# A two-layer graph kernel: the sort split by family, the hub's deal moved forward, layer 1 summed in PSUM

## The chip, the cores and the metric

The kernel runs on one core of one Trainium2 chip. The metric is the device time of one execution in microseconds; the median of three executions before the change is 1130.66 us (1130.05 to 1131.23). The profiled execution took 1129.26 us, with a span of 1127.5 us between its first and last instruction.

## The reference

The inputs are 2708 rows of 1024 float32 numbers (`x`) and a 2708 by 2708 adjacency matrix `adj` of zeros and ones. It is sparse: its rows have between none and a few hundred neighbours, most of them a handful.

```python
# layer 0: attention over the neighbours
q = x @ W_q.T + b_q;  k = x @ W_k.T + b_k;  v = x @ W_v.T + b_v
z = (1 / 32) * (q @ k.T)
z = where(z * adj == 0, -10000, z * adj)
x = layernorm(x + relu(softmax(z, axis=1) @ v))
# layer 1: a sum over the neighbours, then a linear layer
x = layernorm(x + adj @ (x @ W) + bias)
```

`layernorm` takes the mean and the variance over the 1024 numbers of a row, with no weights.

## The kernel before, in words

The kernel uses the sparsity. It finds for each row the list of its neighbours, sorts the rows by their number of neighbours, and handles them in 22 blocks of 128 rows; the rows of a block then have about the same number of neighbours. `SLOTS[b]` is the number of neighbours that block `b` has room for. Instead of dense products over all rows, a block gathers row `j` of each of its members by an indirect DMA (128 rows of 4 KB, 0.52 MB), once for each slot.

The unsorted rows fall in two families, sorted each for itself: the first 1024 rows (`FAMILY = 8` blocks, 0 to 7, slots 15 down to 2) and the other 14 blocks (8 to 21, slots 13 down to 0). Rows with very many neighbours ("hub" rows, at most 32) do not fit 15 slots: their neighbours are dealt out over 128 shares of 11 slots each (`HUB_SLOTS`), handled as one more block called "hub" and added to block 0.

The stages, by the order of TensorE's work:

1. The weights are transposed, and `M = W_q.T W_k` is formed (L293, 256 records). A score between two rows is then `(x_i M) . x_j`. `m_sb` holds M.
2. Beside M, `list_columns` finds the neighbours of one block of rows, in unsorted order: VectorE multiplies the rows of `adj` with the column numbers (L217) and takes the largest eight of a range at a time (MAX8, L220 and L222, with replacements L224). 15 of the 22 lists (`EARLY`) are done in M's loop, the others two at a time ahead of a y block.
3. `sort_begin` (L374 to L394) counts, and puts each row in a class by its number of neighbours (L389, then one-hot columns `hot_f`, L393). `sort_end` (L396 to L433) asks TensorE for the running counts (two products, L398 and L400), works out each row's place, and stores each row's record (its neighbours, own number and degree) at that place: 22 indirect scatters of GpSimd into `tab_d` (L428). `tabs` is that table, read back (L433). `records_back` (L435 to L451) derives from it which slots are valid, one slot per instruction (L446, L447, L450, L451): `valid` is 1 or 0, and `less` is 0 or -1e30, which is added to scores.
4. `y_block(b)` computes `y = x M` for 128 rows (L337, 48 records, about 13.85 us), adds a row vector on the way out of PSUM (`yo`, L341) and stores it. The first eight come before any attention, the other 14 between attention steps.
5. The attention of a block is a "job", cut in pieces of at most six slots (`attend`, `run_job`): gather the block's y rows and its neighbours' x rows, one dot product each on VectorE (L593), a softmax over the slots, and the weighted sum of the gathered rows into `r` (L648 for the first, L650 for the others). A step "v" then transposes `r` (`flip`, L521) and multiplies it with `W_v` (L544, 32 records); `finish0` adds bias (L686), relu and residual, normalises (`norm`, L574 to L589) and scatters the finished rows to `x1_d`. The list `steps` sets the order of y blocks and v steps, the lists `jobs` and `late_jobs` that of the attention. How many jobs go ahead of a step is set by a running account (`credit`) of estimated VectorE time.
6. `deal_hub` (L711 to L837) deals out the hub rows. It is a generator: each `next(deal)` emits one part of it, at the start of that loop and in steps 0, 4, 5 and 7 (L960). Its main cost is on VectorE: the neighbours of the hub rows are found eight at a time out of 677 columns (L751, L753), and the place of each slot by comparison (L801). TensorE adds counts (L779), and GpSimd gathers `found`, eleven times.
7. Layer 1 takes the blocks in pairs (`units`, L1133). `sum_rows` (L1035) gathers the neighbours out of `x1_d` and sums them on VectorE: the first one scaled by its mask (L1044), the others by a multiply-add (L1046). `turn1` transposes both sums of a pair and forms four differences `S` (L1071 to L1074). `work1` multiplies with W by the Strassen-Winograd scheme: seven half products instead of eight, each of eight records (L1079) into a PSUM bank of its own. The combination of the seven, and the bias, is done by VectorE adds of 512 columns (L1101, L1121, L1125, L1126) with ScalarE copying the first product (L1100). `finish1` adds the residual row `xr` and sums up for the mean in one instruction (L1055), normalises, and scatters to the output. In turn `i` of the loop the sums of unit `i + 2` are begun.

[...] GpSimd issues all gathers and scatters, so a scatter whose rows are not ready holds up the gathers behind it. Where the kernel says `follow(a, b)`, instruction `a` is placed behind `b`; `high_priority` moves an instruction ahead in the scheduler that sets the order within each engine. `p_o` is a pool of PSUM banks of 128 x 512, called `po`.

Of the kernel before, what the change touches and what calls it, by code (L numbers as in the profile page):

```python
# [20 lines left out]
P = 128  # L21
# [58 lines left out]
def sparse_part(ctx, tc, x, xT, adj, wqT, wkT, wvT, bq, bk, bv, w1, b1, out):  # L80
# [23 lines left out]
    tab_d = dram.tile([NBP, REC], I32, name="tab_d")  # L104
# [6 lines left out]
    with es:  # L111
# [61 lines left out]
        own = lists.tile([P, NB], F32, name="own")  # L173

# [24 lines left out]
        loaded, sorted_ = [], []  # L199
# [83 lines left out]

        m_sb = wm_pool.tile([P, DC, YW], F32, name="m_sb", tag="m")
        nc.vector.memset(m_sb[:, :, D:], 0.0)
        nc.vector.tensor_copy(m_sb[:, :, D], u_col)
        done = 0
        for i in range(DC):
            for h in range(NH):
                hs = slice(h * HALF, (h + 1) * HALF)  # L290
                po = p_o.tile([P, HALF], F32, name="po")
                for o in range(DC):
                    nc.tensor.matmul(po, wq_o[:, o, i * P:(i + 1) * P], wk_o[:, o, hs],  # L293
                                     start=(o == 0), stop=(o == DC - 1))
                nc.scalar.copy(m_sb[:, i, hs], po)
                while done < EARLY * (i * NH + h + 1) // (DC * NH):
                    list_columns()
                    done += 1
        y_bc = xa.tile([P, YW], F32, name="y_bc", bufs=1)
        bcast_rows(y_bc, y_col)  # L300
        mm = p_mm.tile([P, HALF], F32, name="mm")
        nc.tensor.matmul(mm[:, :1], ones, bqk, start=True, stop=True)
        nc.vector.memset(y_bc[:, D:], 0.0)
        nc.vector.tensor_copy(y_bc[:, D:D + 1], mm[:, :1])

# [54 lines left out]
        products = []  # L360
# [3 lines left out]
        NKB = NK * NB  # L364
        deg = lists.tile([P, NB], F32, name="deg")
        hot_f = lists.tile([P, NKB], F32, name="hot_f")
        families = [(0, FAMILY), (FAMILY, NB - FAMILY)]

        def by_class(t, b0, nb):

            return t[:, NK * b0:NK * (b0 + nb)].rearrange("p (k b) -> p k b", b=nb)


        def sort_begin():  # L374
            got = lists.tile([P, NB, KEYS], F32, name="got")
            nc.vector.tensor_scalar(got, keys, 0.0, None, op0=ALU.is_gt)
            capn = lists.tile([P, NB], F32, name="capn")
            nc.vector.tensor_reduce(capn, got, AX.X, ALU.add)
            nc.vector.tensor_tensor(capn, capn, cnt, op=ALU.not_equal)
            nc.vector.scalar_tensor_tensor(deg, capn, 10000.0, cnt, op0=ALU.mult, op1=ALU.add)  # L380
            nc.vector.tensor_scalar(capn, neg, 0.0, 1.0e6, op0=ALU.is_gt, op1=ALU.mult)
            nc.vector.tensor_add(deg, deg, capn)

            past = lists.tile([P, NB], F32, name="past")
            nc.vector.tensor_scalar(past, own, float(N), float(NK - 2), op0=ALU.is_ge, op1=ALU.add)
            kk = lists.tile([P, NB], F32, name="kk")
            nc.vector.memset(kk, 0.0)
            for least in CLASSES:
                nc.vector.scalar_tensor_tensor(kk, deg, float(least), kk, op0=ALU.is_ge, op1=ALU.add)  # L389
            nc.vector.tensor_sub(kk, past, kk)  # L390
            for k in range(NK):
                for b0, nb in families:
                    nc.vector.tensor_scalar(by_class(hot_f, b0, nb)[:, k, :], kk[:, b0:b0 + nb], float(k), None,  # L393
                                            op0=ALU.is_equal)  # L394

        def sort_end():  # L396
            before = p_mm.tile([P, HALF], F32, name="mm")
            nc.tensor.matmul(before[:, :NKB], lower, hot_f, start=True, stop=True)  # L398
            total = p_tr.tile([P, 4, P], F32, name="tr").rearrange("p a b -> p (a b)")
            nc.tensor.matmul(total[:, :NKB], ones, hot_f, start=True, stop=True)  # L400
            one_row = lists.tile([P, NKB], F32, name="one_row")
            nc.vector.memset(one_row, 1.0)
            upto = lists.tile([P, NKB], F32, name="upto")
# [3 lines left out]
            nc.vector.tensor_mul(upto, upto, hot_f)  # L407
            pos = lists.tile([P, NB], F32, name="pos")
            for b0, nb in families:
                nc.vector.tensor_reduce(pos[:, b0:b0 + nb], by_class(upto, b0, nb).rearrange("p k b -> p b k"),  # L410
                                        AX.X, ALU.add)
            pos_i = lists.tile([P, NB], I32, name="pos_i")
            nc.vector.tensor_copy(pos_i, pos)  # L413

            rec = lists.tile([P, NB, REC], I32, name="rec")
            nc.vector.memset(rec[:, :, ROW:], 0)
            own1 = lists.tile([P, NB], F32, name="own1")
            nc.vector.tensor_scalar_add(own1, own, 1.0)
            fill = lists.tile([P, NB, ROW], F32, name="fill")
            nc.vector.scalar_tensor_tensor(fill, keys, 0.0, own1.unsqueeze(2).to_broadcast([P, NB, ROW]),  # L420
                                           op0=ALU.is_equal, op1=ALU.mult)
            nc.vector.scalar_tensor_tensor(rec[:, :, 0:ROW], keys, -1.0, fill, op0=ALU.add, op1=ALU.add)
            nc.vector.tensor_copy(rec[:, :, ROW], own)
            nc.vector.tensor_copy(rec[:, :, DEG], deg)
            for b0, nb in families:
                nc.vector.tensor_scalar_add(rec[:, b0:b0 + nb, OFF], own[:, b0:b0 + nb], float(-b0 * P))
            for b in range(NB):
                put = nc.gpsimd.indirect_dma_start(  # L428
                    out=tab_d[:, :], out_offset=bass.IndirectOffsetOnAxis(ap=pos_i[:, b:b + 1], axis=0),
                    in_=rec[:, b, :], in_offset=None)  # L430
                tc.declare_no_dep(put.ins, group="tab", reason="disjoint rows: positions are unique")
                tc.add_to_no_dep_group("tab", put.ins)
            nc.gpsimd.dma_start(out=tabs, in_=tab_d.rearrange("(b p) e -> p b e", p=P))  # L433

        def records_back():  # L435

            put = nc.vector.tensor_copy(tab0, tabs[:, 0, :])
            follow(put, products[-1])
            nc.gpsimd.dma_start(out=tab0[:HUB, :J0], in_=tab_d[HUB:2 * HUB, ROW - J0:ROW])
            nc.gpsimd.dma_start(out=tab0[:HUB, :ROW - J0], in_=tab_d[HUB:2 * HUB, J0:ROW])  # L440
            nc.gpsimd.dma_start(out=tab0[:HUB, ROW:], in_=tab_d[HUB:2 * HUB, ROW:])
            deg0 = lists.tile([P, 1], F32, name="deg0")
            nc.vector.tensor_copy(deg0, tab0[:, DEG:DEG + 1])
            nc.vector.tensor_scalar_add(deg0[:HUB], deg0[:HUB], float(-J0))
            for j in range(J0):
                nc.vector.tensor_scalar(valid0[:, j:j + 1], deg0, float(j), None, op0=ALU.is_gt)  # L446
                nc.vector.tensor_scalar(less0[:, j:j + 1], deg0, float(j), -FAR, op0=ALU.is_le, op1=ALU.mult)  # L447
            nc.vector.tensor_copy(degs, tabs[:, :, DEG])
            for j in range(max(SLOTS[1:])):
                nc.vector.tensor_scalar(valid[:, :, j], degs, float(j), None, op0=ALU.is_gt)  # L450
                nc.vector.tensor_scalar(less[:, :, j], degs, float(j), -FAR, op0=ALU.is_le, op1=ALU.mult)  # L451


        for b in range(FAMILY):
            while done < min(NB, EARLY + 2 * (b + 1)):
                list_columns()
                done += 1
            y_block(b)
            if b == FAMILY - DC // 2 - 3:
                wv_sb = wv_pool.tile([P, DC, D], F32, name="wv_sb", tag="v")  # L460
            elif FAMILY - DC // 2 - 2 <= b < FAMILY - 2:
                for c in range(2 * (b - FAMILY + DC // 2 + 2), 2 * (b - FAMILY + DC // 2 + 2) + 2):
                    put = nc.sync.dma_start(out=wv_sb[:, c, :], in_=wvT[c * P:(c + 1) * P, :])
                    follow(put, products[-2])
            if done == NB and b < FAMILY - 1 and not sorted_:
                sort_begin()
                sort_end()
                sorted_.append(b)
            if sorted_ and b == sorted_[0] + 2:
                records_back()  # L470
# [9 lines left out]
        bias_bc = hp.tile([P, D], F32, name="bias_bc", tag="bias")  # L480
        junkv = hp.tile([P, D], U8, name="junkv")
# [7 lines left out]

        def gather_at(src, at, n, dst):  # L490
            nc.gpsimd.indirect_dma_start(out=dst[:n], out_offset=None, in_=src,  # L491
                                         in_offset=bass.IndirectOffsetOnAxis(ap=at, axis=0))
            return dst
# [56 lines left out]
        def project_mean(rT, w):  # L550
# [7 lines left out]
            quarters = hp.tile([P, D // G], F32, name="quarters", tag="a0")  # L558
# [12 lines left out]
        def norm(t, sm, n):  # L571
# [907 lines left out]
```

## Time and profile before

| what | us | where it is from |
|---|---|---|
| median time | 1130.66 | three executions |
| TensorE busy | 1043.0 of 1127.5 | profile, part 1 |
| VectorE busy | 838.4 | profile, part 1 |
| ScalarE, GpSimd busy | 410.9, 450.4 | profile, part 1 |
| first y block starts | 136.83 | timeline |
| first attention score starts | 287.1 | instructions of L593 |
| first pair of layer 1 starts | 831.5 | timeline |
| last matmul ends | 1108.1 | timeline |

In the views, PE is TensorE, PEld its weight loads, DVE VectorE, ACT ScalarE and POOL GpSimd. A window line gives the busy time of each engine within a stretch (with the number of instructions in brackets), then the granted TensorE clock as a share of full speed, the busy share of the 16 DMA engines, and GB/s. A line of waits reads: the engine, its output and line, what it waited for, then the total in us, how often, and the longest. A timeline line gives start, duration, engine, line and operation; brackets at its end hold the idle time ahead of it and what ended it.

### The profile page before, as it was taken

To read this page: it belongs to the slowest core of one execution; us is meant where nothing else is said; L and a number is where in the kernel's file an instruction comes from. 1 tells how busy PE (TensorE), PEld (TensorE's weight loads), DVE (VectorE), ACT (ScalarE), POOL (GpSimd) and SP (SyncE) were. 2 spreads that over 40 slices of the span, in tenths; PEclk is the share of its full clock that TensorE was granted. 3 is DMA by queue.
4 is the path that set the end of the run, shared out by engine and by line. 5 is a ranking of instruction groups with operands and counts; after the bars stand their busy time and mean duration, and the time that the engine had idled before them with its cause. 6 is when DMAs were issued, how large, how long until landed. Compare 5 with 4: busy or idle time off the path is not lost.

```text
span 1127.5 us, 10542 instructions
## 1 busy us (share of the span) xinstructions
PE 1043.0 (93%) x3229; PEld 554.6 (49%) x3229; DVE 838.4 (74%) x1775; ACT 410.9 (36%) x881; POOL 450.4 (40%) x387
## 2 busy tenths in 40 slices
PE   7999999899899798989999999999499999799893
PEld 6444466556555454555654444444244444344341
DVE  7899999505899689982166599952388989999752
ACT  4688887111223023232343243342222322232222
POOL 1000000264245654641056267320375876776410
PEclk9999999899999998999999999999699999999897
DMA  9555567448577467854078589520497888988511
GB/s 366 186 197 203 215 217 224 128 96 309 189 246 248 137 223 267 274 190 167 27 240 298 175 306 305 175 101 31 160 313 264 308 288 304 336 304 320 171 72 40
DMA packets 83041, 243.06 MB, mean 216 GB/s; under 512 B 9164, under 2 KB 31132, under 8 KB 80268
## 3 DMA queue, kind: packets, MB, share of 16 engines
q0 software_dynamic: 48704, 172.90, 44.7%
q1 hardware_dynamic: 34272, 69.40, 18.1%
q8 instruction: 27, 0.44, 0.2%
q14 instruction: 38, 0.31, 0.1%
HBM read 208.59 MB, written 33.68 MB: 215 GB/s over the span
## 4 chain that ended last, share of the span: by engine, by line
PE 41%; DVE 27%; issue 16%; DMA 7%; POOL 6%; ACT 2%; POOLq 0%; DVEq 0%; SPq 0%
PE po L544 15%; PE po L1079 14%; PE po L337 7%; DVE a L217 6%; DVE few L220 5%; DVE junkv L593 2%; POOL g L491 2%; PE tr L521 2%; DVE r L1046 2%; POOL tab_d L428 2%; DVE r L650 2%; DMA g<-in_x_dram,tabs 1%; PE tr L242 1%; DVE yo L341 1%; DMA g<-in_x_dram,tab 1%
## 5 line engine op out<-in xcount | busy, mean ns | idle before, releaser
L337 PE MATMUL po<-m_sb,xt 128*128 128x343 f32 (+1 forms) x1008 | 299.2, 458 | 11.3 <-DVE yo L341 7.7
L544 PE MATMUL po<-wv_sb,rT 128*128 128x512 f32 x672 | 296.4, 600 | 10.0 <-DVE t L686 6.6
L337 PEld LDWEIGHTS po<-m_sb,xt 128*128 128x128 f32 x1008 | 192.9, 192 | 114.3 <-DVE yo L341 8.8
L544 PEld LDWEIGHTS po<-wv_sb,rT 128*128 128x128 f32 x672 | 128.0, 193 | 165.9 <-issue 162.3
L593 DVE SCALAR_TENSOR_TENSOR junkv<-yg,g 128x1024 uint8<-128x1024 f32 x109 | 133.1, 1221 | 38.5 <-DMA yg<-y_d,tabs 20.5
L491 POOL DMA_INDIRECT g<-in_x_dram,tabs x86 | 99.8, 1161 | 91.4 <-DVE yo L328 28.4
L491 POOL DMA_INDIRECT g<-x_d,tabs x83 | 105.6, 1272 | 31.2 <-issue 21.0
L293 PE MATMUL po<-wk_o,wq_o 128*128 128x512 f32 x256 | 110.4, 592 | 0.0
L576 ACT ACTIVATE junks<-t,lnm 128x1024 uint8<-128x1024 f32 (+1 forms) x44 | 50.6, 1150 | 160.7 <-DVE lnm L574 159.4
L1046 DVE SCALAR_TENSOR_TENSOR r<-g,valid,r 128x1024 f32<-128x1024 f32 x77 | 97.7, 1278 | 0.6 <-DMA g<-x_d,tabs 0.5
L1079 PE MATMUL po<-w_sb,rT 128*128 128x512 f32 x192 | 92.3, 628 | 5.5 <-DVE u L1121 5.5
L522 ACT COPY rT<-tr 128x512 f32<-128x512 f32 x80 | 42.4, 587 | 147.8 <-PE tr L521 120.2
L350 ACT ACTIVATE junka<-xt 128x128 f32<-128x128 f32 x176 | 54.0, 307 | 116.0 <-issue 56.7
L428 POOL DMA_INDIRECT tab_d<-rec,pos_i x22 | 21.3, 969 | 185.1 <-DVE pos_i L413 178.7
L650 DVE SCALAR_TENSOR_TENSOR r<-g,pr,r 128x1024 f32<-128x1024 f32 x64 | 81.9, 1280 | 1.3 <-ACT r L648 0.9
L589 ACT ACTIVATE t<-t,nmr,rstd 128x1024 f32<-128x1024 f32 (+1 forms) x44 | 54.5, 1239 | 68.4 <-DVE nmr L588 64.8
L220 DVE MAX8 few<-a 128x8 f32<-128x75 f32 (+3 forms) x132 | 79.0, 617 | 0.1
L293 PEld LDWEIGHTS po<-wk_o,wq_o 128*128 128x128 f32 x256 | 48.4, 190 | 59.8 <-issue 59.6
L1079 PE MATMUL po<-t,s 128*128 128x512 f32 x160 | 72.3, 592 | 0.0
L1079 PE MATMUL po<-w_sb,s 128*128 128x512 f32 x160 | 71.9, 592 | 0.0
L217 DVE SCALAR_TENSOR_TENSOR a<-a,iota 128x2708 f32<-128x2708 f32 (+1 forms) x22 | 65.2, 2962 | 3.8 <-ACT junk L216 3.8
L686 DVE TENSOR_TENSOR t<-po,bias_bc 128x512 f32<-128x512 f32 (+1 forms) x44 | 30.2, 686 | 49.2 <-PE po L544 48.5
(323 smaller groups left out, 1251.3 us busy)
## 6 DMA issues: line engine op xcount, KB each, us to landing
a<-in_adj_dram SPq DMA_DIRECT2D x21, 1354.0 KB, 5.8
y_d<-yo SPq DMA_DIRECT2D x21, 514.0 KB, 5.5
xt<-in_xT_dram SPq DMA_DIRECT2D x21, 512.0 KB, 5.2
wq_i<-in_wqT_dram SPq DMA_DIRECT2D x8, 512.0 KB, 4.5
wk_i<-in_wkT_dram SPq DMA_DIRECT2D x8, 512.0 KB, 10.5
wv_sb<-in_wvT_dram SPq DMA_DIRECT2D x8, 512.0 KB, 5.3
w_sb<-in_w_dram SPq DMA_DIRECT2D x8, 512.0 KB, 3.3
g<-in_x_dram,tabs POOLq DMA_INDIRECT x86, 6.0
```

The costliest lines, as they stand in the source:

```text
L217: nc.vector.scalar_tensor_tensor(a[:n], a[:n], 1.0, iota[:n], op0=ALU.is_equal, op1=ALU.mult)
L220: nc.vector.max(few[:n, i * 8:(i + 1) * 8], a[:n, cuts[i]:cuts[i + 1]])
L293: nc.tensor.matmul(po, wq_o[:, o, i * P:(i + 1) * P], wk_o[:, o, hs], start=(o == 0), stop=(o == DC - 1))
L337: put = nc.tensor.matmul(po[:, :k1 - k0], xt[:, c, :], m_sb[:, c, k0:k1], start=(c == 0), stop=(c == DC - 1))
L350: put = nc.scalar.activation(junka, xts[b][:, c, :], AF.Copy, accum_out=xs[:, c, b:b + 1])
L491: nc.gpsimd.indirect_dma_start(out=dst[:n], out_offset=None, in_=src, in_offset=bass.IndirectOffsetOnAxis(ap=at, axis=0))
L544: put = nc.tensor.matmul(acc, rT[:, c, :], w[:, c, h * HALF:(h + 1) * HALF], start=(c == 0), stop=(c == DC - 1))
L589: nc.scalar.activation(t[:n], t[:n], AF.Identity, bias=nmr[:n], scale=rstd[:n])
L593: nc.vector.scalar_tensor_tensor(junkv[:n], yg[:n, :D], scale, xg[:n], op0=ALU.mult, op1=ALU.mult, accum_out=s)
L650: nc.vector.scalar_tensor_tensor(r[:n], xg[j][:n], pr[:n, j:j + 1], r[:n], op0=ALU.mult, op1=ALU.add)
L1046: nc.vector.scalar_tensor_tensor(r[:n], xg[:n], ok[:n, j:j + 1], r[:n], op0=ALU.mult, op1=ALU.add)
L1079: nc.tensor.matmul(acc, a[:, k], w[:, k], start=start and k == 0, stop=stop and k == DC // 2 - 1)
```

## The change

It has four parts.

First, the sort is done for each family by itself. `sort_begin(f)`, `sort_end(f)` and `records_back(f)` take a family's number, and there are two tables `tab_ds`. The first family is listed after eight lists, and its sort is emitted inside M's loop, after lists 9 and 11; the second family's comes after y blocks 4 and 5. So the table of the first family is there before the first y block.

Second, `deal_hub` needs only the first family's table. It is emitted beside the first eight y blocks, with its small tiles in the memory of the lists.

Third, the masks are made by two instructions per table over all slots at once, by comparing the degree with a row of slot numbers (`places`).

Fourth, layer 1 lets PSUM add. A half product that other sums need goes on accumulating in its bank (`pa`, `pc`): VectorE reads the bank in the middle of the group, and the next half product is added on top. The residual row comes with the bias already in it: ScalarE copies the bias to `xr`, and the gather adds the rows on top (an accumulating DMA). The last addition of each half also gives the sum for the mean (`accum_out`), so the full-width instruction of `finish1` goes. The first gathered row is scaled by ScalarE, except in units 0 and 1. Sums are begun three units ahead instead of two, hub's in turn 4 instead of 5, and the units have a new order.

```diff
-        def sort_begin():
+        def sort_begin(f):
...
+                    if done == FAMILY + 1:
+                        sort_begin(0)
+                if not sorted_ and done > FAMILY + 2:
+                    sort_end(0)
+                    sorted_.append(0)
...
+        deal = deal_hub()
         for b in range(FAMILY):
             while done < min(NB, EARLY + 2 * (b + 1)):
                 list_columns()
                 done += 1
             y_block(b)
+            if b in (0, 1, 3, 4, 5, 6):
+                next(deal)
...
+            if b == FAMILY - 4:
+                sort_begin(1)
+            if b == FAMILY - 3:
+                sort_end(1)
+            if b == 0:
+                records_back(0)
+        records_back(1)
...
+        def masks(ok, less_, d):
+            put = nc.vector.tensor_tensor(ok, *of, op=ALU.is_lt)
+            nc.vector.tensor_scalar(less_, ok, FAR, -FAR, op0=ALU.mult, op1=ALU.add)
...
-            for j in range(max(SLOTS[1:])):
-                nc.vector.tensor_scalar(valid[:, :, j], degs, float(j), None, op0=ALU.is_gt)
-                nc.vector.tensor_scalar(less[:, :, j], degs, float(j), -FAR, op0=ALU.is_le, op1=ALU.mult)
...
-            if i in (0, 4, 5, 7):
-                next(deal)
...
+        units = [(20,), (19, 18), (17, 16), (15, 1), (14, 2), (7, 8), (9, 3), (4, 10), (6, 0), (5, 11), (12, 13)]
-        units = [(20,), (19, 18), (17, 16), (15, 7), (14, 8), (13, 6), (12, 5), (9, 4), (1, 11), (0, 10), (2, 3)]
...
-                    firsts.append(nc.vector.tensor_scalar(r[:n], xg[:n], ok[:n, 0:1], None, op0=ALU.mult))
+                    if b in units[0] + units[1]:
+                        firsts.append(nc.vector.tensor_scalar(r[:n], xg[:n], ok[:n, 0:1], None, op0=ALU.mult))
+                    else:
+                        nc.scalar.activation(r[:n], xg[:n], AF.Copy, scale=ok[:n, 0:1])
...
+        def gather_x1(b, k=0):
+            nc.scalar.copy(xr[:n], bias1[:n])
+            return gather_at(x1_d[:, :], tabs[:n, b, ROW:ROW + 1], n, xr, ALU.add)
...
-            nc.vector.scalar_tensor_tensor(t[:n], t[:n], 1.0, xr[:n], op0=ALU.mult, op1=ALU.add, accum_out=sm[:n])
-            norm(t, sm, n)
-            if b in units[-1]:
-                nc.gpsimd.tensor_copy(idle[:n], sm[:n])
+            norm(t, sums[0], n, sums[1])
...
-            part_of(S[1], t2, (u, u))
-            part_of(S[0], t1, (v, u))
-            nc.vector.tensor_add(v, v, bh)
-            nc.vector.tensor_add(u, u, bl)
-            part_of(S[2], t3, (ts[1][:, HALF:], v), (u, u))
-            part_of(S[3], w22, (ts[0][:, HALF:], v))
-            part_of(a12, w21, (ts[0][:, :HALF], low))
-            part_of(a22, t4, (ts[1][:, :HALF], u))
+            half_products(pa, a11, w11, stop=False)
+            add(x0[0], pa, x0[0])
+            half_products(pc, S[0], t1, stop=False)
+            add(x1[1], pc, x1[1])
+            half_products(pa, S[1], t2, start=False, stop=False)
+            add(x0[1], pa, x0[1])
+            pb = bank()
+            half_products(pb, a12, w21)
+            whole(0, 0, pb, x0[0])
+            half_products(pa, S[2], t3, start=False, stop=False)
+            whole(1, 1, pa, x1[1])
+            half_products(pc, S[3], w22, start=False)
+            whole(0, 1, pc, x0[1])
+            half_products(pa, a22, t4, start=False)
+            whole(1, 0, pa, x1[0])
...
-            if i + 2 < len(units):
-                got1[i + 2] = [sum_rows(b) for b in units[i + 2]]
-            if i == 5:
+            if i + 3 < len(units):
+                got1[i + 3] = [sum_rows(b, k) for k, b in enumerate(units[i + 3])]
+            if i == 4:
                 sum_rows("hub")
```

`add` is a VectorE addition and `whole` a multiply-add with a row sum, both of 512 columns.

## The prediction

> **What bounds the kernel now.** I read busy times first, then stretches by stage, then the waits of TensorE, then the timeline around a long wait.
>
> ```profile
> PE 1043.0 (93%) x3229; PEld 554.6 (49%) x3229; DVE 838.4 (74%) x1775; ACT 410.9 (36%) x881; POOL 450.4 (40%) x387
> ```
>
> TensorE is the bound: of 1127.5 us it idles 84.5. About 6 of these lie ahead of its first work, 19.9 after its last matmul (1108.1), and 58 in between. Only the middle part, and the clock lost around it, can be won, since the change takes no product out of TensorE.
>
> ```profile
> core 0: us, PE busy (x) PEld busy (x) DVE busy (x) ACT busy (x) POOL busy (x), PEclk, DMA share, GB/s
> 137.00:287.00 150.00, 139.99 (x468) 90.34 (x467) 94.22 (x303) 64.13 (x177) 39.85 (x42) 0.97 0.61 192
> 287.00:490.00 203.00, 185.45 (x568) 106.36 (x568) 179.94 (x360) 51.49 (x182) 103.15 (x85) 0.95 0.67 223
> 490.00:805.00 315.00, 302.40 (x999) 155.00 (x999) 183.43 (x408) 108.29 (x263) 111.00 (x93) 0.99 0.54 182
> 830.00:930.00 100.00, 100.00 (x280) 47.73 (x279) 85.97 (x146) 32.99 (x60) 73.71 (x58) 1.00 0.84 290
> 930.00:1060.00 130.00, 116.89 (x337) 56.76 (x336) 123.76 (x184) 34.98 (x63) 90.45 (x72) 0.95 0.85 299
> ```
>
> Two stretches stand out. From 287 (the first attention score) to 490, VectorE is busy 180 of 203 us and TensorE loses 17.5 us and a twentieth of its clock. In layer 1, 930 to 1060, VectorE is busy 124 of 130 and TensorE loses 13; but the DMA engines are at 0.85 there too. The waits name the partner.
>
> ```profile
> engine line waited for: us in total, times, longest us
> PE tr L521 <- DVE r L1044: 15.0, 1, 15.0
> PE po L337 <- DVE yo L341: 7.7, 2, 4.2
> PE tr L521 <- DVE r L1046: 7.6, 3, 3.2
> PE po L544 <- DVE t L686: 6.6, 1, 6.6
> PE po L1079 <- DVE u L1121: 5.5, 2, 3.0
> PE mm L398 <- DVE hot_f L393: 4.2, 1, 4.2
> PE mm L779 <- DVE more L776: 3.0, 1, 3.0
> ```
>
> The 15.0 is the change-over to layer 1 (the last layer-0 rows must be stored before they are gathered) and nothing here touches it. The two layer-1 rows, 7.6 and 5.5, are the 13 us above. A stall costs more than its length:
>
> ```profile
> 1049.34 6.39 PE L1079 MATMUL po<-w_sb,rT 128*128 128x512 f32 x8 [2.44 <-DVE u L1121]
> 1055.57 3.60 PE L1079 MATMUL po<-t,rT 128*128 128x512 f32 x8
> ```
>
> The same eight records take 3.60 us in the stream and 6.39 after the wait, so 2.8 us more per long stall. Two such in layer 1 make 5 us.
>
> **What the Trainium skill says.** "TensorE: Matmul & The Clock Gate", Part 1, says that an idle window of about 3.4 us puts TensorE at half clock until it has been busy for about as long; the 6.39 against 3.60 agrees. "PSUM — Partial Sum Buffer", The four PSUM rules, allows a synchronised read of a partial sum inside an accumulation group, and its collision section asks for a semaphore per bank: each mid-group read becomes a wait for TensorE. No run here shows it yet. "DMA: Bandwidth & Descriptors", Rules for kernel authors, says that an accumulating DMA reads its destination and writes it later, and must wait for what touched these bytes before; it gives no price, and no transfer of this kernel accumulates. The price of an fp32 add in "VectorE: DVE Perf Modes" ((N+151)/0.96 ns, 691 ns for 512 columns) agrees with the adds of L1121 at 680 to 685 ns.
>
> **Part 1, sorts and masks by family.** Small VectorE operations cost nearly the same for fewer columns (17 of L389, 182 ns; 38 of L393, 162 ns), so sorting twice adds the class chain again and half of the rest: about 5.7 us. The 26 mask operations of 195 and 191 ns (L450, L451) and the 30 of 145 ns (L446, L447), 8.6 us, become six broadcast ones; the widest has 14 blocks x 13 = 182 columns or 8 x 11, and by L405 (418 columns, 581 ns) they cost 0.2 to 0.45 each, so about -5 us net of gaps. Together nothing. TensorE's two small products of the first sort fall into M, about +0.6 us.
>
> **Part 2, hub's deal beside the first y blocks.** What moves on VectorE: ten MAX8 (862 ns), nine replacements (851 + 89), L746 (866), eleven of L801 (342 + 79) and some 60 small ones at about 0.16: with gaps about 40 us. It leaves 287 to 490 (in part; some was at 252 to 287) and enters a stretch where VectorE is full until 199 with the lists: per block L217 2.96 us and the MAX8 group, 6.8 us, 150 us for 22. I added up VectorE's queue in the changed order from the first list at 43.7: 150 of lists, 36.8 of sort and hub, 8.6 of y adds, so the second sort's classes are ready at 238. TensorE's small product for it stands inside y block 6, reached at about 230. So TensorE stalls 8 to 10 there. Then eleven `found` gathers and fourteen scatters at 1.27 us stand in a row on GpSimd, the records land at about 279, and VectorE waits for them at `degs` after the last y add: about 4 us more. Before, this stretch lost 10 (140 of 150) and some clock. Part 2 therefore gives nothing before 287: -5 to +5, taken 0.
>
> In 287 to 490 VectorE's queue falls from 186 us (issue to issue, from the first score to the last add of y block 16) to about 170, and TensorE's own work at full clock is about 180. TensorE becomes the longer queue, but transfers still come late at times (VectorE waits 20.5 us for `yg`). Of the 22 us between 180 and 202 I take 12 as won, range 0 to 17.
>
> 490 to 805: the same instructions on TensorE, 302 of 315; nothing.
>
> **Part 3, layer 1.** VectorE per pair of blocks: 8 adds at 0.62 to 0.69 out of PSUM, 3 adds of bias, two L1055 (1219), two first rows L1044 (768), 10.5 us issue to issue; after, 3 adds and 4 half-width multiply-adds with sums, about 4.5. That is 6.1 us x 10, some 60 us of 240. ScalarE gains two bias copies and two first rows (each like L576, 1.15) and loses the 0.57 of L1100: +4 us per 25.8 us pair, with ScalarE at 33 of 100: hidden.
>
> A pair is 7 half products of 3.43 us and 1.77 of flips: 25.8. Without stalls the first pair at 831.5 would lead to a last matmul at about 1090, against 1108.1: 18 to be won, 13 idle and 5 clock. What can take it back is the order of units: block 0 (15 gathers) and hub (11) stand in unit 8, not 9. Counting GpSimd's queue, 119 transfers of 0.52 MB must land before block 0's flip, which TensorE reaches at about 993. Before, about 103 were issued at 979, with the DMA engines at 0.93 in 950 to 980. Going on at the measured 1.65 us each, the last lands at about 1003. Some 9 us can be made up in 830 to 920, where the DMA share was 0.80 to 0.87. So a stall of 2 to 11, taken as 7, with 2.5 for the clock.
>
> The accumulating gathers: 22, of which 12 or so before that point. Lower bound nothing; upper bound a second transfer, 1.65 each, 20 us. I take a fifth, inside the 7. The bank that is reused must be read by VectorE within one half product (3.43 us): an add of 0.68 behind a running 1.28 leaves about 1.4 us. While a sum waits for a gather this slack goes; I put 2 us. Layer 1: 18 - 7 - 2.5 - 2 = about 7.
>
> **Part 4, tail.** L1055 (1.22) and the idle copies leave the last block's path, a half-width operation enters: -1.5.
>
> **Sum.** 12 + 7 + 1.5 - 0.6 = 20: 1130.7 - 20 = about 1110.
>
> **Rivals.** (a) Both reliefs in full: 17 in 287 to 490, 15 in layer 1, 1.5: 1097. For it: VectorE was the named partner everywhere; against it: the DMA share. 0.20. (b) The front gives nothing, because 40 us more of hub and sort in a full VectorE delay y blocks and the first score by some 12 us: 20 - 12, 1122. For it: 30.00 busy of 30 in 137 to 167. Against it: TensorE's PSUM leaves it about 15 us of slack against late y adds. 0.17. (c) Slower: accumulation doubles its transfers (20 us more at block 0's flip) and mid-group reads stall each pair by 1 us (10): layer 1 goes from +7 to -23, and the rest gives 13: 1140. For it: DMA at 0.92; a VectorE queue held by a late gather now holds TensorE's only free bank. 0.15. My forecast: 0.48.
>
> **Range.** The lower end takes in most of (a), 1092; the upper end (b) and a part of (c), 1131. Faster by over 0.2% (below 1128.4): forecast, (a), (b), less a little: 0.80; same 0.06; slower 0.14.
>
> **What would show it.** The wait on L393's classes grows from 4.2 to 8 or more, and one on `degs` appears; 287 to 490 holds more y work per us and VectorE is under 85% busy; in layer 1 VectorE falls under 80% and `u` waits vanish, while one wait of TensorE for block 0's sum, ended by a gather, appears in unit 7. I am wrong if accumulating gathers land visibly later than plain ones, if TensorE waits in each pair for a PSUM read, or if the first score comes later than 290.

## The result, and the profile after

The changed kernel takes 1114.31 us (median of four, 1109.76 to 1117.78), against 1130.36 before (one execution more than in the table ahead): a ratio of 0.9855 with a 95% interval of 0.9818 to 0.9891. The forecast was 1110, so 20 us less; it is 16. Its executions lie 8 us apart, those of before 1.2.

The profiled execution is the fastest, 1109.76 us, 19.6 us of span less than before. Part 1 and three stretches of the changed kernel, with the same columns as for the kernel before. The line numbers of a view are those of the kernel that it shows.

```profile
PE 1034.6 (93%) x3233; PEld 550.8 (50%) x3233; DVE 783.6 (71%) x1711; ACT 445.6 (40%) x915; POOL 454.9 (41%) x388
```

```profile
137.00:287.00 150.00, 145.27 (x503) 93.98 (x502) 111.56 (x329) 68.09 (x180) 51.48 (x53) 0.99 0.64 204
287.00:490.00 203.00, 190.54 (x597) 109.65 (x597) 170.71 (x300) 60.55 (x221) 100.42 (x76) 0.98 0.72 238
930.00:1060.00 130.00, 127.38 (x374) 62.29 (x373) 91.75 (x164) 55.11 (x87) 84.19 (x67) 1.00 0.87 286
```

TensorE's idle time falls from 84.5 to 73.3 us (11.2), and its busy time from 1043.0 to 1034.6 (8.4), with the same large products and a few small ones more: they run at a better clock. The trace's clock records show half clock in pieces of 3.41 us or multiples of it. Without the 17.07 us at the change-over, which both kernels have, they add up to 30.7 us before and 13.7 after ahead of layer 1, and to 13.7 and 3.4 within layer 1. VectorE drops from 124 to 92 us in 930 to 1060.

Where in time the gain lies, from the first starts of the lines concerned:

| event | before | after | gained so far |
|---|---|---|---|
| first y block starts | 136.8 | 141.7 | -4.9 |
| first score starts | 287.1 | 281.4 | 5.7 |
| last layer-0 product starts | 795.1 | 781.4 | 13.7 |
| first layer-1 product starts | 812.5 | 799.8 | 12.7 |
| last layer-1 records start | 1107.5 | 1087.8 | 19.7 |
| end of the span | 1127.5 | 1107.9 | 19.6 |

TensorE's waits after (line 684 is the transposes, 685 ScalarE's copies of them, 318 the y product, 322 its adds, 527 the sort's product):

```profile
PE tr L684 <- DVE r L1063: 15.9, 1, 15.9
PE tr L684 <- ACT rT L685: 10.3, 3, 4.9
PE po L318 <- DVE t L852: 5.2, 3, 4.0
PE po L318 <- DVE yo L322: 4.2, 4, 2.3
...
PE mm L527 <- DVE hot L521: 2.6, 2, 2.3
```

The waits for `u` and for the sums of L1046 in layer 1 are gone, and no wait for a mid-group read has come. The change-over is as it was. New is the second line: transposes of layer 1 wait for ScalarE. What held ScalarE shows in its own timeline ahead of the wait that ends at 879.36:

```profile
873.89 1.15 ACT L1065 ACTIVATE r<-g,valid 128x1024 f32<-128x1024 f32 x1 [11.53 <-DMA g<-x_d,tabs]
876.74 1.15 ACT L1065 ACTIVATE r<-g,valid 128x1024 f32<-128x1024 f32 x1 [1.70 <-DMA g<-x_d,tabs]
877.79 1.03 ACT L1074 COPY xr<-bias 128x1024 f32<-128x1024 f32 x1
878.73 2.03 ACT L685 COPY rT<-tr 128x512 f32<-128x512 f32 x4
```

The scaling of a first row stands for 11.53 us at the head of ScalarE's queue, waiting for a gather. Behind it are the copies (L685) of a transposition that is needed now. The transposes wait 2.71 us for them. ScalarE does not pass the waiting instruction by: in both profiles of the changed kernel its 915 instructions stand in the same order, although their times differ by up to 4 us.

### The profile page after: what moved, and what is told of

It is laid out like the page before. It is cut to its first block, busy times and chain, and to the rows that moved or that the text cites. A ratio compares the mean times of both kernels' runs of the same rounds, so it can differ in the third digit from the quotient of the medians.

```text
span 1107.9 us, 10505 instructions
## 1 busy us (share of the span) xinstructions
PE 1034.6 (93%) x3233; PEld 550.8 (50%) x3233; DVE 783.6 (71%) x1711; ACT 445.6 (40%) x915; POOL 454.9 (41%) x388
## 4 chain that ended last, share of the span: by engine, by line
PE 43%; DVE 21%; issue 16%; DMA 8%; POOL 8%; ACT 2%; POOLq 0%; DVEq 0%
PE po L707 16%; PE po L1101 14%; PE po L318 6%; DVE few L224 5%; DVE a L221 4%; DMA g<-x_d,tabs 3%; DVE junkv L759 3%; POOL g L342 3%; DMA g<-in_x_dram,tabs 2%; PE tr L684 2%; PE po L598 2%; POOL tab_d L554 1%; PE tr L246 1%; POOL found L342 1%; DVE r L816 1%
## 5 line engine op out<-in xcount | busy, mean ns | idle before, releaser
L707 PE MATMUL po<-wv_sb,rT 128*128 128x512 f32 x672 | 292.1, 593 | 5.9 <-DVE nm L877 2.2
L342 POOL DMA_INDIRECT g<-x_d,tabs x83 | 92.5, 1115 | 27.6 <-issue 19.2
L1101 PE MATMUL po<-w_sb,rT 128*128 128x512 f32 x192 | 88.9, 606 | 0.0
L554 POOL DMA_INDIRECT tab_d<-rec,pos_i x22 | 25.1, 1139 | 129.6 <-DVE pos_i L540 123.1
L684 PE MATMUL tr<-ident,r 128*128 128x128 f32 x320 | 42.9, 281 | 28.2 <-DVE r L1063 15.9
L219 ACT ACTIVATE junk<-a 128x2708 uint8<-128x2708 f32 (+1 forms) x22 | 54.1, 2459 | 24.1 <-DMA a<-in_adj_dram 19.3
```

Source lines behind the costliest of these rows:

```text
L219: nc.scalar.activation(junk[:n], a[:n], AF.Sign, accum_out=cnt[:n, b:b + 1])
L684: nc.tensor.transpose(tr[:, k, :], r[:, c * P:(c + 1) * P], ident)
L707: put = nc.tensor.matmul(acc, rT[:, c, :], w[:, c, h * HALF:(h + 1) * HALF], start=(c == 0), stop=(c == DC - 1))
L1101: nc.tensor.matmul(acc, a[:, k], w[:, k], start=start and k == 0, stop=stop and k == DC // 2 - 1, skip_group_check=True)
```

## The experiments

Twelve measurements on three chips, each with the kernel before beside it on the same chip (1129.83, 1130.04 and 1132.71 us). Ratios are to that; kernels are compared on one chip, or by their ratios.

**The two halves alone.** The front (sorts, masks, deal) with the old layer 1, and the new layer 1 behind the old front; the parts of the diff shown ahead of the prediction, nothing else. (Where VectorE and ScalarE do the front's work, their order is that of the changed kernel but for a few neighbours; on GpSimd nine of the first attention gathers stand ahead of the hub's transfers, so this front is not quite that of the changed kernel.)

> The sorts by family, the masks and the hub's deal of the change, with the layer 1 of before. Theory (gain is spread: 12 to 13 us in front, 7 in layer 1): 1130.4 - 12.5 = about 1118, with the last layer-0 product ending near 782 and a layer 1 of 295 us. Rival (the parts need each other): over 1124, or under 1112 if layer 1 gives nothing.

> The layer 1 of the change behind the front of before. Theory: 1130.4 - 7 = about 1123, with the same three waits of TensorE for the copies of transposed sums (10 us in all) in layer 1. Rival: 1130 or slower, if the accumulating gathers and the new order only pay with the new front; 1115 or less if the front was what gave nothing.

Measured: the front alone 1115.61 us, ratio 0.9872 (0.9850 to 0.9893), so 14 us less; layer 1 alone 1128.90, ratio 0.9993 (0.9982 to 1.0004), so 0.9 less. In their profiles layer 1, from its first to its last product, takes 295.1 us in the first and 289.6 in the second. The second is 5.4 us shorter than before, and the expected waits for the copies of transposes are there (9.0 us). But the front of this execution, whose instructions stand in the old order, ended 4.3 us later (last layer-0 product at 799.4), with 37.5 us of half clock in it instead of 30.7. Why the shorter layer 1 shows so little in the times stays open. Most of the gain is the front's.

**The changed kernel again**, unedited.

> The changed kernel as it is, for its spread: its four times lay between 1109.8 and 1117.8, where before lay within 1.2 us. Theory (layer 1 now hangs on the landing of gathers, which varies): again 5 to 8 us of spread, and where the profiled execution is slow, layer 1 is the longer part and the front the same. Rival: the front varies, or the spread does not come back.

Measured: 1112.33 us (1109.68 to 1117.89), ratio 0.9856 (0.9832 to 0.9879): the spread came back. The profiled execution was again the shortest, 1109.68 us, so the parts of the longer ones were not seen. The two profiles differ in the clock: 13.7 and 3.4 us of half clock (front and layer 1) in the first, 10.2 and 10.2 in this one, and the parts move by 2 us each. That the number of 3.41-us pieces makes the spread is likely, but not shown.

**First rows of layer 1 back on VectorE.**

```diff
-                    if b in units[0] + units[1]:
-                        firsts.append(nc.vector.tensor_scalar(r[:n], xg[:n], ok[:n, 0:1], None, op0=ALU.mult))
-                    else:
-                        nc.scalar.activation(r[:n], xg[:n], AF.Copy, scale=ok[:n, 0:1])
+                    firsts.append(nc.vector.tensor_scalar(r[:n], xg[:n], ok[:n, 0:1], None, op0=ALU.mult))
```

> The changed kernel with every first gathered row of layer 1 scaled by VectorE again. Theory A (ScalarE's queue is the new bound: its scaling of a first row waits for the gather, and the copies that TensorE's transposes need stand behind it; 10.3 us of waits): these waits go, 5 to 9 us less than the changed kernel in the same call, near 1106. Theory B (the DMA engines set the pace; the wait only moves to the sum on VectorE): within 2 us of the changed kernel. Theory C (14 us more on VectorE bring its waits back): 3 to 8 us slower.

Measured: 1115.51 us, ratio 0.9870 (0.9849 to 0.9892), not faster than the 0.9856 beside it. Theory A as put has fallen; the median lies 3.2 us above, the way Theory C put it, but the intervals overlap. ScalarE's waits and TensorE's, both in layer 1:

```profile
ACT xr L1071 <- DVE t L1121: 75.7, 7, 15.6
```

```profile
PE tr L684 <- ACT rT L685: 8.9, 2, 4.6
PE po L1098 <- DVE xr L1116: 2.6, 3, 1.8
```

Another waiting instruction now stands at the head of ScalarE's queue: the bias copy, which waits for its residual buffer to come free. And mid-group reads begin to be late (second line of TensorE).

**Copies of transposes ahead, in ScalarE's queue.** Two versions: bias copies and first rows both placed behind the latest copies, and bias copies so placed with the first rows on VectorE.

```diff
+                        follow(nc.scalar.activation(r[:n], xg[:n], AF.Copy, scale=ok[:n, 0:1]), copies[-1], same=True)
...
+            follow(nc.scalar.copy(xr[:n], bias1[:n]), copies[-1], same=True)
```

> The changed kernel with ScalarE's bias copies and first rows of layer 1 placed behind the copies of the latest transposes. Theory B (ScalarE's in-order queue): TensorE's waits for these copies, 10 us in layer 1, fall to under 5, the time by 3 to 6 us. Theory A (gathers come late anyway): the wait moves to the sums, time within 2 us.

> First rows of layer 1 on VectorE and the bias copies behind the copies of transposes, so that nothing in ScalarE's queue ahead of these copies waits for a gather or for a residual buffer. Theory B: no wait of TensorE for ScalarE is left in layer 1 beyond the first pair, and 4 to 8 us less than the changed kernel. Theory C (VectorE then holds the mid-group reads): waits of TensorE for the reads of PSUM of 1 to 2 us each appear, and the gain is under 3 us.

Measured: 1113.69 us, ratio 0.9857 (0.9838 to 0.9877), and 1115.42, 0.9869 (0.9849 to 0.9890). Neither gains. In the first TensorE's waits for the copies are 11.0 us: the first rows of a later unit still stand ahead of the next unit's copies. In the second they are 7.0, with 4.4 for mid-group reads; there the normalisation of an earlier unit heads ScalarE's queue, and waits for the row mean (`lnm`) that VectorE works out:

```profile
853.70 1.15 ACT L744 ACTIVATE junks<-t,lnm 128x1024 uint8<-128x1024 f32 x1 [17.58 <-DVE lnm L742]
```

Reordering moves this wait and does not remove it.

**Plain gathers of the residual rows.** ScalarE's bias copies stay, so that its queue is the same; the gather overwrites them, and the bias of layer 1 is left out.

```diff
-            return gather_at(x1_d[:, :], tabs[:n, b, ROW:ROW + 1], n, xr, ALU.add)
+            return gather_at(x1_d[:, :], tabs[:n, b, ROW:ROW + 1], n, xr)
```

> The changed kernel with the 22 gathers of residual rows in layer 1 made plain instead of accumulating; ScalarE still copies the bias, the gather then overwrites it, so the bias of layer 1 is left out of the result. In 830 to 1060 the changed kernel spends 88.5% of the DMA engines on 66.4 MB, before 84.0% on 67.8 MB: about 14 us of DMA time for 19 accumulating gathers, 0.75 each. Theory A (the DMA pace sets layer 1): DMA share falls to about 0.83 and the time by 4 to 8 us. Theory B (the in-order queue of ScalarE is what TensorE waits for): the share falls as well, the time stays within 2 us.

Measured: 1101.82 us, ratio 0.9744 (0.9719 to 0.9768), 11 to 13 us less than the changed kernel, and so more than Theory A put. Layer 1 takes 279.0 us, 9 less than in the changed kernel and 9.6 less than in the kernel with the late deal, measured on the same chip. The order of the instructions on VectorE, ScalarE and GpSimd is that of the changed kernel throughout. The DMA view of 830 to 1060, of the changed kernel and then of this one (MB and share of the queue; then for each gather the median us from issue to landing):

```profile
q0 software_dynamic: 18286, 66.36, 88.5%
...
g<-x_d,tabs POOLq DMA_INDIRECT x63, 7.6
xr<-x_d,tabs POOLq DMA_INDIRECT x19, 7.4
```

```profile
q0 software_dynamic: 18226, 66.16, 80.9%
...
g<-x_d,tabs POOLq DMA_INDIRECT x63, 6.2
xr<-x_d,tabs POOLq DMA_INDIRECT x19, 6.0
```

The bytes are the same and the share falls by 7.6% of 230 us, 17.5 us: 0.9 us for each of 19 accumulating gathers, about half of a transfer of 1.65. The 63 gathers of sorted blocks land 1.4 us earlier too in the median (1.0 against the second profile of the changed kernel, 7.2); block 0's fifteen land 0.6 us earlier, the hub's do not. TensorE's waits in layer 1 fall from 10.3 us to:

```profile
PE tr L684 <- ACT rT L685: 2.3, 2, 1.4
PE po L1101 <- DVE xr L1119: 0.4, 1, 0.4
```

No half clock is left in layer 1. So the accumulating DMA is shown to be the cause, and about 8 of the 9 us are waits of TensorE for ScalarE's copies. That late gathers bring them about, by a first row that waits with copies behind it, is read from the timelines of these waits.

**The hub's deal at its old place.** Sorts, masks and layer 1 as changed; the deal's small tiles have memory of their own again.

```diff
-            if b in (0, 1, 3, 4, 5, 6):
-                next(deal)
...
+            if i in (0, 4, 5, 7):
+                next(deal)
+            if i == 7:
+                next(deal)
```

> The changed kernel with the hub's deal put back behind the first eight y blocks (steps 0, 4, 5, 7), sorts by family and masks as changed. Theory (the deal's 40 us of VectorE were what TensorE waited for between the first score and y block 16): 8 to 12 us slower than the changed kernel, with more half-clock time of TensorE in 290 to 450. Rival (the early table of the first family and the masks gave the gain): within 3 us of it.

Measured: 1110.36 us (1109.65 to 1111.80), ratio 0.9828 (0.9811 to 0.9845). It is not slower than the changed kernel, rather 2 or 3 us faster, though the intervals overlap. The stretch from 220 to 290 of the kernel before and of the changed kernel, then the stretches of this one:

```profile
220.00:290.00 70.00, 62.29 (x210) 40.23 (x209) 20.63 (x99) 12.00 (x60) 38.03 (x41) 0.98 0.60 192
220.00:290.00 70.00, 66.81 (x228) 43.02 (x227) 32.18 (x159) 11.99 (x61) 41.43 (x42) 0.98 0.59 188
```

```profile
137.00:220.00 83.00, 83.00 (x291) 54.06 (x290) 76.18 (x204) 57.33 (x127) 20.59 (x19) 1.00 0.75 262
220.00:290.00 70.00, 70.00 (x245) 46.20 (x244) 39.16 (x86) 18.84 (x86) 29.29 (x28) 1.00 0.60 181
287.00:490.00 203.00, 186.20 (x582) 106.93 (x581) 172.03 (x348) 53.41 (x193) 105.00 (x86) 0.96 0.68 225
```

TensorE does not idle at all from 137 to 290, and the first score starts at 267.1, 20 us ahead of before and 14 ahead of the changed kernel. Part of that is given back between 287 and 490, where TensorE waits 10.2 us at once for a `t` add behind the deal, and runs 17.1 us at half clock (6.8 in the changed kernel). From the first score to the last layer-0 product this kernel takes 513.7 us, the changed kernel 500.0 and the kernel before 508.0. At the last layer-0 product the two are level: 780.8 and 781.4.

**The masks alone**, in the kernel before. With its two tables these are four broadcast operations for the 56, not six as expected below; the changed kernel with three tables has six.

> The kernel before with the masks alone made as changed: six broadcast operations for 56 small ones. The deal's place gave nothing (deal at its old place: 1110.4), so the 14 us of the front are of the sorts or of the masks. Theory (the sort of the first family, which ends VectorE's wait for the tables, gave it): masks alone 0 to 4 us faster than before. Rival (the masks, which stand right ahead of the first score): 6 us or more.

Measured: 1130.26 against 1132.71 us, ratio 0.9980 (0.9972 to 0.9988): 2.3 us; the first score comes 2.4 us earlier, at 284.7. What is left of the front's 14 is the sort by family, by difference some 12 us if the deal's place is worth nothing. No kernel had the sort alone.

**The bias by other ways.** Bias laid into the PSUM banks by ScalarE, with plain gathers; the same with the deal at its old place; and the bias added to the gathered rows by VectorE. ScalarE's bias copies into `xr` go in all three (but for the last block in the first two).

```diff
+            return gather_at(x1_d[:, :], tabs[:n, b, ROW:ROW + 1], n, xr)
...
-            pa, pc = bank(), bank()
-            half_products(pa, a11, w11, stop=False)
+            pa, pc = bank(bias1[:, :HALF]), bank(bdiff)
+            half_products(pa, a11, w11, start=False, stop=False)
```

```diff
+            gather_at(x1_d[:, :], tabs[:n, b, ROW:ROW + 1], n, xr)
+            nc.vector.tensor_add(xr[:n], xr[:n], bias1[:n])
```

> The changed kernel with plain gathers of the residual rows in layer 1 (but for the last block) and the bias laid into the banks by ScalarE ahead of their first half product: the low half into pa, high minus low into pc, so that each sum has its own bias once. Nothing is left out. Theory (the accumulating gathers were the cost): layer 1 of about 279 to 282 us as with plain gathers, time near 1103. Rival (each bank must now be free for ScalarE's copy before TensorE may use it): waits of TensorE for these copies, 1 us or more in each pair, and 1110 or over.

> Bias in the banks and plain gathers as in the first of these, and the hub's deal at its old place. Theory (the two are independent, and the deal's place is worth -2 to +2): 1100 to 1104, the fastest or level with the fastest so far. Rival: the earlier first score brings late stalls, over 1105.

> The changed kernel with plain gathers of the residual rows and the bias added to them by VectorE, 1.2 us a block, 26 us in all. Nothing is left out. VectorE is busy 168 of 230 us in 830 to 1060 in the changed kernel. Theory (VectorE has room since the PSUM sums): within 3 us of plain gathers without bias, 1102 to 1106. Rival (these adds wait for a gather in VectorE's queue and hold the mid-group reads): 1108 or over, with waits of TensorE for reads of PSUM.

Measured: 1129.62 us, ratio 0.9977 (0.9962 to 0.9991); 1114.37, 0.9831 (0.9812 to 0.9851); 1126.36, 0.9943 (0.9921 to 0.9964). None keeps the 12 us of the plain gathers. (One of 13 executions of the first took 2848.92 us; it is not in the ratio and not explained here.) In layer 1 the banks cost what the gathers saved, 293.3 and 297.0 us against 288.0 to 290.0 of the changed kernel. The copy into a bank waits in ScalarE's queue for a read of that bank (28.7 us of ScalarE's waits in the first, up to 1060). The transposes wait 7.5 and 7.9 us, and again behind a first row that waits for its gather, though the gathers are plain:

```profile
940.05 1.15 ACT L1067 ACTIVATE r<-g,valid 128x1024 f32<-128x1024 f32 x1 [9.28 <-DMA g<-x_d,tabs]
```

In both, TensorE also stands 3.2 us at one place of layer 1 (before 1018 and 1007) for nothing that the trace names; that is not explained. With VectorE's adds layer 1 takes 285.7 us, 2 to 4 us less than in the changed kernel, with 3.3 us of waits for the copies and 2.9 for mid-group reads.

But the first and the third are slow by their front, whose instructions stand in the order of the changed kernel: the first scores start at 293.8 and 296.3, not 281 to 283. From 253 to 275 TensorE's records of the first of them come one by one:

```profile
253.68 0.45 PE L318 MATMUL po<-m_sb,xt 128*128 128x343 f32 x1 [0.26 <-issue]
255.78 0.45 PE L318 MATMUL po<-m_sb,xt 128*128 128x343 f32 x1 [1.65 <-issue]
257.88 0.73 PE L318 MATMUL po<-m_sb,xt 128*128 128x343 f32 x1 [1.65 <-issue]
```

Half of the records or more are missing, the steps are multiples of 0.70 us where 0.288 is normal, the trace names nothing that is waited for, and 20.5 us of half clock begin at 257.9. The third kernel shows the same from 254 to 279; the second, on the same chip, does not. What holds TensorE up there is open; so a total of these two says nothing on their layer 1.

## Why the prediction was right, and where not

The sum was near: 20 forecast, 16 by the times, 19.6 in the profile. Its two large terms came out for reasons other than those given, so that the sum is near is in part luck. One of the signs of being wrong came too: accumulating gathers land later than plain ones, 7.4 us against 6.0.

- **"TensorE is the bound ... only the middle part, and the clock lost around it, can be won."** Right: TensorE is busy for 93% of the span before and after, and 8.4 of the 19.6 us are clock. The 6.39 against 3.60 us was set beside an idle window of about 3.4 us; the wait in that line is 2.44 us, so shorter waits cost clock here as well.
- **"Together nothing" for sorts and masks.** Wrong, and the chief error. I counted instructions and not when their results are there. Masks gave 2.3 us, the sort by family about 12 by difference. Before, VectorE stood 18.4 us for the tables and was busy only 20.6 of 70 us from 220 to 290. With the first family's table there before the first y block, the first score can start 20 us earlier, 2.4 of them by the masks, as the kernel with the late deal shows. In the changed kernel a wait for the second family's table is left. The two waits, before and after:

```profile
DVE tab L437 <- DMA tabs<-tab_d: 18.4, 1, 18.4
```

```profile
DVE degs L584 <- DMA tabs<-tab_d: 16.9, 1, 16.9
```

- **"Part 2 therefore gives nothing before 287", and "of the 22 us between 180 and 202 I take 12 as won".** The 12 seemed to come (13.7 us in the profile at the end of layer 0, 14 by the times), but by two errors that offset each other. From the first score on, the deal's leaving is worth 8 us against the kernel before and 14 against the kernel with the late deal, much as forecast. Ahead of the first score it was put at nothing, and costs 14 us: 281.4 with it there, 267.1 without. So its move gives nothing in all; what is won is the early table, which was put at nothing. Rival (b), a first score some 12 us late, had the price of the deal about right and missed the same gain of the sort.
- **"TensorE stalls 8 to 10 there", for the second sort.** It stalled 0.2 us (236.78 in the trace). The classes were ready at about 237, as worked out, but TensorE came there just then: its first y block began 4.9 us late, and a product of the deal cost it a wait of 1.5. I had 0.6 for the first of these: M waited 2.3 us for the first sort and, in this profile, ran 3.4 us at half clock. The wait on `degs` came as forecast, 16.9 us on VectorE; the y adds behind it and behind the first score cost TensorE 2.8.
- **Layer 1, "18 - 7 - 2.5 - 2 = about 7".** 7.0 in the profile, but the terms taken off were others. The stall for block 0 did not come. Mid-group reads cost nothing. The accumulating gathers, put at "a fifth" of a transfer, "inside the 7", cost 0.9 us of DMA time each, about half of one, and 9 us of layer 1 in all: 279.0 without, 288.0 with. They are the mis-sized term; without them layer 1 is 16.0 us shorter than before, close to the 18. The rule in the Trainium skill ("DMA: Bandwidth & Descriptors", Rules for kernel authors) that such a DMA reads its destination and writes it later gave the direction; the half of a transfer is what the runs add. The times give layer 1 less than the profile, 0.9 us alone and 3.3 on top of the front (1115.61 to 1112.33 on one chip), and neither is clear of the noise. So the 4 us by which the median misses the forecast may lie here; this is not settled.
- **ScalarE "hidden".** Its busy time is; its queue is not. This wait was in none of my cases.
- **Tail -1.5.** Nothing in this profile, 20.0 us and 20.1 from the last records to the end; the kernels with the new layer 1 lie between 18.6 and 20.2.

## What to carry to other kernels

A change in when a result is there can be worth more than the work it adds: look for the stretch where the busy engine of the next stage stands idle and follow its longest wait back. When work is moved into such a gap, price it there too, and not only at the place that it leaves. Before work is moved to an engine with time to spare, ask what each moved instruction waits for and what stands behind it, since a busy share of 40% said nothing here of a queue whose head waited for a gather. And where the DMA engines are as busy as here, at 0.88, price an accumulating transfer against an add on an engine with a plain gather.

## What the runs showed of the hardware

- An accumulating indirect gather of 128 rows of 4 KB costs about 0.9 us of the 16 DMA engines above a plain one here (88.5% against 80.9% of 230 us, 19 gathers), and lands 1.0 to 1.4 us later in the median (7.0 and 7.4 in two profiles of the changed kernel, 6.0 for plain ones in their place). Its issue on GpSimd takes 1.63 us in the median, against 1.44 for those plain ones and 0.95 for the plain ones of the kernel before.
- VectorE read PSUM in the middle of an accumulation group, with one half product of 3.43 us between the read and the next use of the bank, and TensorE lost nothing by it while VectorE was busy 168 of 230 us (830 to 1060). With the first rows back on VectorE it was busy 176 and 179, and such waits came, up to 1.8 and 3.3 us each.
- TensorE's clock fell to half for 3.41 us or a multiple of it in these traces. The same wait of 2.07 us ahead of the same sixteen transposes, at 567 to 587, did this in some executions and not in others: they took 1.96 or 1.97 us in five profiles (both of the changed kernel among them) and 2.81 to 3.44 in six.
